# The softmax sums' inverse and division, done at the end of the first slot of a group of four

## The chip, the cores and the metric

The kernel runs on one core of a Trainium2 chip. The metric is the device time of one execution in microseconds (us); lower is better. Below, PE is TensorE, DVE is VectorE, ACT is ScalarE, POOL is GpSimd and SP is SyncE, as the profile names them. L416 is line 416 of the kernel.

## The reference

One block of a conditioned transformer over x of 4 x 1024 x 512, all in fp32: attention with 16 heads of 32, then a gated feed-forward network with 2048 hidden features, and x added once more.

```
def _attention(x, Wq, Wk, Wv, Wo):
    q, k, v = (x @ W.T for each W).reshape(B, L, H, dh)
    attn = jnp.einsum('blhd,bmhd->bhlm', q, k) / scale
    p = jax.nn.softmax(attn, axis=-1)
    o = jnp.einsum('bhlm,bmhd->blhd', p, v).reshape(B, L, D)
    return o @ Wo.T

x = x + _attention(_tc_rmsnorm(x, t, g1w, g1b, b1w, b1b), Wq, Wk, Wv, Wo)
block = x + silu(n @ gate_w.T) * (n @ hid_w.T) @ out_w.T   # n = _tc_rmsnorm(x, t, g2w, ...)
out = x_in + block
```

The change lies in the last step of the softmax: the division of the weighted values by the sum of the exponentials.

## The kernel before, in words

The 4096 tokens are 8 blocks of 512. The attention of a block is 8 groups, each 4 heads by 256 queries over all 1024 keys; a group is 4 slots of 256 keys. So there are 64 groups and 256 slots, and the main loop (L768) runs over a slot number g. I call g % 4 the kind of a slot (0 to 3), the four slots from one of kind 0 a group of slots, and number the 8 groups of slots of a stretch of 32 by position 0 to 7 (position 0 starts at a multiple of 32).

The order of the instructions on PE, DVE, ACT and POOL is written out by hand (`manual_schedule`): it is the order of the calls in this loop. Only SP's DMAs are put in order by a scheduler. Each engine runs its own list in order; where one stands still, all behind it stand.

What one slot does for the attention, with several slots of the pipeline at once:

- `scores(g)` (L310): 16 matmuls of keys and queries into the PSUM tile `sc`; `keep` (L317, ACT) copies it to an SBUF tile `raw`; `running_max` (L322 and L325, DVE) takes the maximum over the keys, in two halves.
- Once a group, in a slot of kind 0, PE transposes the maximum (`mt`, L331), DVE reduces and splits it (L337 to L342); in the next slot, of kind 1, PE transposes that (`pt`, L347), ACT copies it (L349), PE spreads it over the partitions (`sp`, L357), and ACT copies it to the tile `shift` (L358, two halves).
- `shifted(g-5)` (L363, DVE) subtracts it from `raw`: 2048 columns at the beginning of a slot, in kind 1 two halves that wait for `shift`. `exponential(g-5)` (L366, ACT) follows, and in the next slot `weighted` (L376, PE, `av`) multiplies by the values, and `accumulate` (L390) adds up the exponentials with DMAs issued by POOL.
- Three groups of slots after the group's own, in the slot of kind 0, `fold_sum` (L398, DVE) and `sums` (L408, PE) form the sums, and ACT copies them to the tile `total` (L413).
- `inverse` (L416, DVE) is the reciprocal of `total`, and `normalize` (L425, DVE) multiplies the values `avs` by it into `oT`. Both stand at the end of the slot of kind 2, and so on DVE right ahead of `shifted` of the slot of kind 3. For the last group of a block (`j_n % GB == GB - 1`, position 2) they stand at the end of the slot of kind 0, since the output projection needs `oT` then. For group 8 the multiplication comes later (L791).

From slot 60 (`FS`) on, the feed-forward network of the block before is woven in. Each pair of slots forms one of 16 hidden tiles with seven products (a Strassen scheme in two PSUM banks, `pa` and `pb`): `pair_15` and `add_15` (L524, DVE) in the odd slot, then `pair_26` (PE, `pa`), `copy_156` (L539, ACT), `contract` (`pc`, with `take_contract`, L577, DVE), `pair_7`, `sub_5` (L546, DVE) in the even one, then `pair_3`, `gate_tanh` (L556, ACT), `gate` and `hidden` (L561, L564, DVE). All feed-forward matmuls have line 106, that of the helper `mm`. The output projection of a block (`po`) runs at position 2.

Before slot 60 the keys, queries and values of later blocks are projected instead (`pkq`, `pv`), with the norms of their inputs (the reciprocal L632, 128x512, at the end of slots 4, 12, 20, 28, 36 and 44) and sums of weights (L474 to L477). Work listed in `ended` (norms, token sums, weight sums) stands behind the inverse and the division at the end of its slot.

Of the kernel before, what the change touches and what calls it, by code (L numbers as in the profile page):

```python
# [24 lines left out]
def tile_cond_transformer_block(  # L25
# [389 lines left out]
    def inverse(j: int):  # L415
        nc.vector.reciprocal(state["total", j], state["total", j])  # L416

    def normalize(j: int):

        m, qh = divmod(j, NB // HQ)  # L420
        n, hg = divmod(m, C)
        total = state.pop(("total", j))
        if (n, hg) not in oT:
            oT[n, hg] = sb.tile([P, NB], F32, tag=f"oT{hg}", name=f"oT{m}")
        nc.vector.tensor_tensor(oT[n, hg][:, qh * HQ : (qh + 1) * HQ], avs.pop(j), total, ALU.mult)  # L425
# [157 lines left out]
    GB = C * (NB // HQ)  # L583
# [114 lines left out]
    with tc.manual_schedule(  # L698
# [35 lines left out]
        direct = NR // UN - 2  # L734
# [33 lines left out]
        while g < END:  # L768
            kind = g % UN
# [6 lines left out]
            j_n = g // UN - 3  # L776
            n_on = 0 <= j_n < NR // UN
# [84 lines left out]
            else:  # L862
# [34 lines left out]
                    chain(g)()  # L897
                for fn, a in halfway.pop(g, []):
                    fn(*a)
            if kind == 0 and n_on and j_n < direct and j_n % GB == GB - 1:  # L900
                inverse(j_n)
                normalize(j_n)
            if kind == 2 and n_on and j_n < direct and j_n % GB != GB - 1:

                inverse(j_n)
                if j_n != GB:
                    normalize(j_n)
            columns[0] = DH
# [95 lines left out]
```

## Time and profile before

| | us |
|---|---|
| median of 3 runs (lowest, highest) | 2479.35 (2477.35, 2480.38) |
| the profiled execution | 2480.0 |
| its span | 2478.1 |
| PE idle before `av`, for `raw` from ACT | 50.0, in 61 waits |
| PE idle before `pa`, for `pa` from DVE | 8.5, in 43 waits |
| L416 reciprocal, 64 of them | 111.6, 1.744 each |
| L425 multiplication, 64 of them | 27.2, 0.425 each |

A slot is measured on PE, from its first `sc` matmul to that of the next slot. From slot 64 on, each stretch of 32 slots looks like the last; these are slots 128 to 159:

| position | kind 0 | kind 1 | kind 2 | kind 3 |
|---|---|---|---|---|
| 0 | 10.73 | 6.19 | 8.10 | 5.53 |
| 1 | 10.73 | 6.19 | 8.10 | 5.53 |
| 2 | 10.73 | 13.25 | 8.10 | 12.56 |
| 3 | 9.91 | 7.25 | 8.10 | 5.53 |
| 4 | 10.70 | 6.19 | 9.45 | 5.53 |
| 5 | 10.86 | 6.19 | 8.10 | 5.53 |
| 6 | 11.94 | 6.19 | 8.10 | 5.53 |
| 7 | 12.53 | 6.19 | 8.10 | 5.53 |

Position 2 holds the output projection. Before slot 60 the slots of kind 0 from slot 12 on take 12.43, 10.61, 11.22, 11.28, 10.61, 11.28, 11.22, 10.61, 10.60, 12.27, 10.61 and 10.60 us.

How to read it: the profile's timeline has a start and a duration in us for each instruction, and in brackets how long its engine had stood idle before it and who ended that. Starts are counted from the beginning of the span.

### The profile page before, as it was taken

The page shows a single profiled execution, that of the slowest core. Times are in us where ns is not written, and L with a number is a line of the kernel's source. Part 1 is how long each engine was busy: PE and PEld are TensorE (multiplying, and loading weights), DVE is VectorE, ACT ScalarE, POOL GpSimd, SP SyncE. Part 2 cuts the span into 40 slices and gives each one's busy share as a digit, 9 for nine tenths or more (in the row PEclk, how much of TensorE's full clock was granted, in tenths as well). Part 3 has the DMA queues.
Part 4 walks back from the last instruction along what each step waited for, and adds up shares of the span by engine and source line. Part 5 has one row for each costly group of instructions (what it writes and reads, how often), then busy time and mean ns, then how long its engine had stood idle before and what let it go on. Part 6 is the DMA issues. An engine that isn't in the chain of part 4 may idle for free. (4 is left out here: it accounts for less than half of the span.)

```text
span 2478.1 us, 71138 instructions
## 1 busy us (share of the span) xinstructions
PE 2396.0 (97%) x31785; PEld 1121.8 (45%) x31785; DVE 1943.7 (78%) x2180; ACT 1412.4 (57%) x1495; POOL 172.4 (7%) x207
## 2 busy tenths in 40 slices
PE   8999999999999999999999999999999999999999
PEld 3333333344444444444444444444444444444444
DVE  2688888888789988998899978997899889843332
ACT  3677777766566656665666656665666566512111
POOL 0000000000000000000000000000000000000000
PEclk9999999999999999999999999999999999999999
DMA  6599998989878888888888888788788888853432
GB/s 214 178 299 251 265 259 221 238 201 238 197 193 203 203 218 200 200 211 214 207 197 207 226 191 204 199 226 203 196 201 212 210 197 199 201 159 116 138 134 71
DMA packets 185982, 501.69 MB, mean 202 GB/s; under 512 B 21319, under 2 KB 78663, under 8 KB 158286
## 3 DMA queue, kind: packets, MB, share of 16 engines
q0 software_dynamic: 28656, 208.68, 43.6%
q1 hardware_dynamic: 156734, 288.47, 34.2%
q8 instruction: 250, 4.10, 0.6%
q14 instruction: 54, 0.44, 0.1%
q10 hardware_dynamic: 288, 0.01, 0.0%
HBM read 246.44 MB, written 41.97 MB: 116 GB/s over the span
## 5 line engine op out<-in xcount | busy, mean ns | idle before, releaser
L363 DVE TENSOR_TENSOR raw<-raw,shift 128x2048 f32<-128x2048 f32 (+1 forms) x320 | 593.9, 1859 | 65.2 <-ACT shift L358 62.3
L366 ACT ACTIVATE raw<-raw 128x2048 f32<-128x2048 f32 x256 | 490.8, 1917 | 214.3 <-DVE raw L363 213.8
L317 ACT COPY raw<-sc 128x2048 f32<-128x2048 f32 x256 | 479.6, 1873 | 169.9 <-PE sc L310 129.7
L322 DVE TENSOR_TENSOR rmax<-rmax,raw 128x1024 f32<-128x1024 f32 x384 | 469.5, 1223 | 53.9 <-ACT raw L317 48.2
L106 PE MATMUL pc<-h,ow 128*32 128x512 f32 x4096 | 467.7, 593 | 2.1 <-DMA ow<-in_out_w 1.1
L376 PE MATMUL av<-raw,v 128*32 128x256 f32 x4096 | 274.9, 386 | 50.0 <-ACT raw L366 50.0
L390 POOL DMA_DIRECT2D raw<-raw x192 | 165.3, 861 | 1991.5 <-ACT raw L366 939.1
L310 PE MATMUL sc<-q,k 32*128 32x256 f32 x4096 | 293.3, 400 | 0.2 <-ACT raw L317 0.2
L106 PE MATMUL pa<-x,fa 128*32 128x256 f32 x4096 | 270.0, 381 | 8.8 <-DVE pa L524 8.5
L106 PE MATMUL pa<-sums,fw 128*32 128x256 f32 x4096 | 267.9, 379 | 0.0
L106 PEld LDWEIGHTS pc<-h,ow 128*32 128x32 f32 x4096 | 128.2, 110 | 245.5 <-issue 226.7
L310 PEld LDWEIGHTS sc<-q,k 32*128 32x128 f32 x4096 | 184.9, 184 | 116.5 <-issue 81.5
L106 PE MATMUL pkq<-y,wkq 128*32 128x512 f32 (+1 forms) x1664 | 231.3, 594 | 4.2 <-ACT y L196 4.1
L376 PEld LDWEIGHTS av<-raw,v 128*32 128x32 f32 x4096 | 107.2, 109 | 175.8 <-ACT raw L366 88.0
L106 PEld LDWEIGHTS pa<-x,fa 128*32 128x32 f32 x4096 | 127.6, 110 | 124.7 <-DVE pa L524 30.5
L106 PEld LDWEIGHTS pa<-sums,fw 128*32 128x32 f32 x4096 | 133.2, 110 | 88.2 <-issue 0.5
L539 ACT COPY pb<-pa 128x256 f32<-128x256 f32 x128 | 46.2, 361 | 181.4 <-PE pa L106 180.3
L577 DVE SCALAR_TENSOR_TENSOR res<-pc,res 128x512 f32<-128x512 f32 x128 | 88.2, 689 | 67.2 <-PE pc L106 62.9
L556 ACT ACTIVATE t<-pa 128x512 f32<-128x512 f32 x128 | 78.1, 610 | 109.9 <-PE pa L106 109.5
L106 PE MATMUL pa<-x,fw 128*32 128x256 f32 x2048 | 135.2, 381 | 0.0
L106 PE MATMUL pb<-x,fw 128*32 128x256 f32 x2048 | 134.0, 379 | 1.2 <-ACT pb L539 1.2
L106 PE MATMUL pb<-sums,fa 128*32 128x256 f32 x2048 | 133.9, 379 | 0.0
(106 smaller groups left out, 2152.4 us busy)
## 6 DMA issues: line engine op xcount, KB each, us to landing
raw<-raw POOLq DMA_DIRECT2D x192, 1024.0 KB, 9.1
fw<-sw SPq DMA_DIRECT2D x128, 512.0 KB, 7.0
fa<-in_gh_w SPq DMA_DIRECT2D x128, 384.0 KB, 5.9
ow<-in_out_w SPq DMA_DIRECT2D x128, 256.0 KB, 2.9
wkq<-in_kq_w SPq DMA_DIRECT2D x32, 512.0 KB, 5.9
v<-vs SPq DMA_DIRECT2D x128, 128.0 KB, 5.0
k<-kqs SPq DMA_DIRECT2D x124, 128.0 KB, 7.0
kqs<-st SPq DMA_DIRECT2D x61, 256.0 KB, 7.7
```

What stands on the lines that cost most here:

```text
L106: nc.tensor.matmul(dst[k : k + n, :], w[:, k : k + n], moving, start=start, stop=stop, skip_group_check=seeded)
L310: nc.tensor.matmul(sc[:, i, k, :], keys[rows, k * P : (k + 1) * P], queries[rows, :], start=True, stop=True)
L317: nc.scalar.copy(raw[r].rearrange("p k h q -> p h k q"), state.pop(("sc", r)))
L322: nc.vector.tensor_tensor(rmax[j], rmax[j], raw[r][:, k, :, :], ALU.max)
L363: nc.vector.tensor_tensor(t, t, s.unsqueeze(1).to_broadcast(list(t.shape)), ALU.add)
L366: nc.scalar.activation(raw[r], raw[r], AF.Exp)
L376: nc.tensor.matmul(av[j][i * DH : (i + 1) * DH, :], v[m, u][:, k, i * DH : (i + 1) * DH], raw[r][:, k, i, :], start=(kt == 0), stop=(kt == ...
L390: nc.gpsimd.dma_start(out=acc[j].rearrange("p k h q -> p (k h q)"), in_=raw[r].rearrange("p k h q -> p (k h q)"), accum_op=ALU.add,)
L539: nc.scalar.copy(bank_b[p][:, RIGHT], bank_a[p][:, RIGHT])
L556: nc.scalar.activation(state["t", p], bank_a[p], AF.Tanh, scale=0.5)
L577: nc.vector.scalar_tensor_tensor(r, pp, 0.5, r, ALU.mult, ALU.add)
```

## The change

The inverse and the division of every group that is not one of the last two stand at the end of the slot of kind 0, where they stood before only for the last group of each block. The exception of group 8, whose multiplication comes later, stays.

```
-            if kind == 0 and n_on and j_n < direct and j_n % GB == GB - 1:
+            if kind == 0 and n_on and j_n < direct:
                 inverse(j_n)
-                normalize(j_n)
-            if kind == 2 and n_on and j_n < direct and j_n % GB != GB - 1:
-
-                inverse(j_n)
+
                 if j_n != GB:
                     normalize(j_n)
```

In the built programs, the lists of PE, ACT and POOL are in the same order in both kernels. On DVE 55 reciprocals and 54 multiplications move (of group 8 the reciprocal alone). On SP five DMAs change places, all before slot 60: loads of keys and values ahead of stores of weight sums in slots 13 and 37, and one load of keys by one place.

## The prediction

> **What bounds the kernel now.** The page's first part shows PE nearly always busy:
>
> ```profile
> PE 2396.0 (97%) x31785; PEld 1121.8 (45%) x31785; DVE 1943.7 (78%) x2180; ACT 1412.4 (57%) x1495; POOL 172.4 (7%) x207
> ```
>
> What a change on DVE can win is PE's idle time. I therefore read the waits next, PE's first:
>
> ```profile
> PE av L376 <- ACT raw L366: 50.0, 61, 2.6
> PE pa L106 <- DVE pa L524: 8.5, 43, 0.2
> ```
>
> 58.5 us of PE's 82 idle us (2478.1 - 2396.0) end with an exponential, or with the sum that stands behind the maximum on DVE. Splitting these waits by slot gives 28.0 and 8.3 us to the slots of kind 0 from slot 60 on, 5.4 to those of kind 0 before slot 60, 12.5 to those of kind 2, 4.2 to the slots after the last scores. The timeline shows what a kind-0 wait comes from; slot 103 is of kind 3, position 1. DVE, then ACT, then PE:
>
> ```profile
> 878.33 1.74 DVE L416 RECIPROCAL total<-total 128x256 f32<-128x256 f32 x1
> 880.10 0.42 DVE L425 TENSOR_TENSOR oT<-avs,total 128x256 f32<-128x256 f32 x1
> 880.45 2.29 DVE L363 TENSOR_TENSOR raw<-raw,shift 128x2048 f32<-128x2048 f32 x1
> ```
>
> ```profile
> 882.77 1.91 ACT L366 ACTIVATE raw<-raw 128x2048 f32<-128x2048 f32 x1 [1.34 <-DVE raw L363]
> ```
>
> ```profile
> 883.28 1.15 PE L310 MATMUL sc<-q,k 32*128 32x256 f32 x16
> 884.73 1.07 PE L376 MATMUL av<-raw,v 128*32 128x256 f32 x16 [0.30 <-ACT raw L366]
> ```
>
> The pair stands straight ahead of the subtraction; ACT has idled 1.34 us for it; PE waits for ACT. No instruction between is free to overtake. So the bound is PE, plus once per group the chain DVE, ACT, PE of kind 3.
>
> **What leaves kind 3.** The pair occupies DVE from 878.33 to where the next instruction starts, 880.45: 2.12 us. Without it the subtraction ends at 880.62 instead of 882.74. ACT then waits only for its tanh (880.83 + 0.60), so the exponential starts at 881.43 and ends at 883.34, and PE comes to `av` at 884.36 by itself: 1.0 us to spare. The sum L524 (885.52 to 885.94) moves by 2.12 to 883.82, when PE wants it at 885.24: to spare too.
>
> How much does the slot shrink? The trace has the slot without the pair ahead of it: position 3, since position 2 has its pair in kind 0. The windows view of a kind-0 slot at position 2 (pair in the kind 3 before) and at position 3 (not):
>
> ```profile
> 883.28:894.01 10.73, 10.23 (x134) 4.69 (x130) 10.26 (x15) 6.07 (x6) 0.86 (x1) 1.00 0.97 250
> 927.92:937.83 9.91, 9.91 (x134) 4.87 (x131) 8.38 (x12) 5.55 (x6) 1.72 (x2) 1.00 1.03 231
> ```
>
> Columns: length, then busy PE, PEld, DVE and so on. 134 matmuls in both, DVE 96% busy against 85%. The slot is 0.82 us shorter, of which only 0.50 is recorded idle; PE also looks 0.32 us busier after a wait. I take lengths, not gaps.
>
> [...]
>
> With 9.91 as the free length, the gains of kind 0 by position in the table above are 0.82, 0.82, 0.82, 0, 0.79, 0.95, 2.03. Position 6 (11.94) has two `norm_scale` (1.28 together) behind the pair in kind 2; without the pair its exponential ends at 0.47 into the slot, before PE's 1.08. Position 7 (12.53) has token sums in the chain; there `fold_sum` would end about 4.24 us into the slot, where PE wants it at 3.69, so I take 9.91 + 0.65 = 10.56 and a gain of 1.97. Sum per 32 slots: 8.20.
>
> **What arrives in kind 1.** The end of a kind-0 slot on DVE is followed by the subtraction of kind 1, in two halves. DVE, slot 101 (no pair) and slot 105 (position 2, pair already there):
>
> ```profile
> 865.52 2.50 DVE L363 TENSOR_TENSOR raw<-raw,shift 128x1024 f32<-128x1024 f32 x2 [1.64 <-ACT shift L358]
> ...
> 894.34 1.74 DVE L416 RECIPROCAL total<-total 128x256 f32<-128x256 f32 x1
> 896.12 0.42 DVE L425 TENSOR_TENSOR oT<-avs,total 128x256 f32<-128x256 f32 x1
> 896.46 1.22 DVE L363 TENSOR_TENSOR raw<-raw,shift 128x1024 f32<-128x1024 f32 x1
> ```
>
> Slot 101 starts at 863.46, slot 105 at 894.01: the subtraction starts 2.06 and 2.45 us in. The idle 1.64 us take most of the pair's 2.12; the two halves end at 4.55 and 4.80. The exponential starts at 5.21 in both (868.67 and 899.22), because ACT copies `sc` and `avs` first. So in a plain group the pair costs nothing, with 0.4 us to spare. This is a measured twin, seven times in the trace.
>
> Not so where other work already fills that idle time, as the pair goes ahead of it. Only what is left of the idle time and the spare before ACT is cover then. PE reaches `av` 1.08 us into kind 2, and the exponential, starting at 5.21, ends 0.96 in: only 0.1 to spare there.
>
> - Position 6: two `norm_scale` (329 to 1611 ns into slot 121). They end at 3.73, the halves at 6.01, the exponential at 7.99, that is 1.80 into kind 2; `av` 0.78 late.
> - Position 7: a token sum (0.68); exponential ends 1.20 in; 0.18 late.
> - Position 3: norm sums, but that slot is 7.25 long; ends 0.94 in; nothing.
> - Position 4's wait of 1.28 in kind 2 is ACT's table load; it stays.
>
> So 0.96 per 32 slots, net 8.20 - 0.96 = 7.24; six stretches (slots 64 to 255): **-43.4**.
>
> **Before slot 60.** Here the end of kind 0 holds the long reciprocal of the norm:
>
> ```profile
> 214.00 3.35 DVE L632 RECIPROCAL tota<-tota 128x512 f32<-128x512 f32 x1
> 217.26 1.16 DVE L363 TENSOR_TENSOR raw<-raw,shift 128x1024 f32<-128x1024 f32 x1
> ```
>
> DVE has no gap left (slot 21 starts at 214.37); the halves end at 5.19, the exponential starts at 5.22. Pushed by 2.12 it ends 3.09 into slot 22, `av` 2.07 late. Slots 12, 20, 28, 36 do this: 2.12 + 2.07 + 2.07 + 2.12. Slot 44 moves the reciprocal alone: 1.6. Slot 48 (weight and norm sums) 1.2, slot 24 (weight sums) 0.36, slots 56 and 60 0.18 and 0.16. Loss 11.9. Gains are the kind-0 slots over the free 10.61: slots 20, 24, 32, 36 by 0.61, 0.67, 0.67, 0.61, slot 48 by 1.66; slot 12's wait has no pair ahead. Gain 4.2. Net **+7.7**.
>
> **After the last scores.** Slot 256 loses its wait of 1.38 and what hangs on it (-1.5); slot 257 has no copies on ACT to hide the pair (+1.15); slot 259 loses 2.1 of its 2.56. Net **-2.4**.
>
> The moved pair issues no DMA. Of the five moved on SP, loads go ahead of stores that would now wait longer; I count nothing, with 2 us either way. On DVE the reciprocal waits for L413, which ends 0.8 us before at the least (slot 48): nothing. `oT` is needed five slots later or more. Sum: -43.4 + 7.7 - 2.4 = -38.1; from the profiled 2480.0, 2441.9, and the median of the runs lies 0.65 below that execution, within its spread. I say **2442**.
>
> [...]
>
> **Rivals.**
>
> [...]
> 2. The slot shrinks only by the recorded gap (0.5, not 0.82): 6 positions by 0.32, six times, 11.5 less: 2454. For it: position 3 follows the long slots of the projection, so DVE starts it with less behind. Against: the same 134 matmuls.
> 3. The early waits are absorbed, since DVE and PE are late by the same amount and kind 2 loses its pair: half of the 11.9 goes, 2436. Against: in these slots PE waits at once.
> 4. Transfers bound instead. DMA share is 0.97 to 1.03 in the rows above, and at position 2 the last accumulation lands 4.1 us before its fold, which the change takes 1.3 earlier. It would need groups to keep their 30.5 us: no change, 2480. Against: PE waits 1.1 us for a DMA in the whole trace.
>
> That nothing moves is excluded by the order of the built programs.
>
> **Numbers.** Forecast 0.65, rival 1 0.06, rival 2 0.16, rival 3 0.09, rival 4 0.04. Range 2432 to 2458: from rival 3 to rival 2, with the 2 us of SP and the 1.5 us by which the runs spread added at both ends. 0.2% (5 us) is what a measurement can tell from no change. Faster 0.90, same 0.04, slower 0.06.
>
> **What would show it.** Right: kind-0 slots of 9.9 us at positions 0 to 6, no `av` wait in them, kind 1 still 6.19; in kind 2 new waits of 0.8 at position 6, and of 2 in slots 14, 22, 30, 38. Wrong: `av` waits in kind 2 of plain positions, reciprocals over 1.75, or `fold_sum` waiting for a DMA.

## The result, and the profile after

| | before | after |
|---|---|---|
| median of the runs, us | 2479.34 | 2451.15 |
| lowest, highest | 2477.35, 2480.38 | 2447.08, 2453.34 |
| the profiled execution | 2480.0 | 2447.08 |
| its span | 2478.1 | 2445.3 |

The ratio of the times is 0.9887, with an interval of 0.9875 to 0.9899. The change wins 28 us where 37 were forecast. The four runs after the change lie 6.3 us apart, at 2447.1, 2449.2, 2453.1 and 2453.3, and the profiled one is the lowest: its trace holds less than the median has to tell.

The page's first part and then the view of waits, PE's rows, of the kernel after (line, what it waited for, us in total, times, longest):

```profile
PE 2386.7 (98%) x31785; PEld 1128.7 (46%) x31785; DVE 1938.9 (79%) x2180; ACT 1416.2 (58%) x1495; POOL 172.8 (7%) x207
```

```profile
PE av L376 <- ACT raw L366: 30.6, 24, 3.5
...
PE av L376 <- ACT totf L151: 3.3, 6, 0.6
```

The waits of `av` for the exponential fell from 50.0 us in 61 times to 30.6 in 24, and PE's wait for `pa` on DVE, 8.5 us before, is down to 0.2. But the longest wait of the first row is now 3.5 us, and a row is new: `av` waits six times 0.55 us for a copy of a norm (L151). The prediction has neither.

The windows view, at slots 104 and 108 (kind 0 of positions 2 and 3, the two slots that the prediction set side by side) and slot 110 (kind 2 of position 3). Columns: length, then busy PE, PEld, DVE, ACT, POOL with instructions, granted PE clock (share of full speed), DMA share, GB/s:

```profile
888.47:898.38 9.91, 9.91 (x134) 4.87 (x130) 8.57 (x13) 4.73 (x5) 0.86 (x1) 1.00 0.92 248
932.29:942.20 9.91, 9.91 (x134) 4.87 (x130) 8.38 (x12) 5.56 (x6) 1.72 (x2) 1.00 1.03 229
949.45:958.17 8.72, 8.17 (x116) 3.74 (x112) 8.06 (x9) 6.18 (x7) 0.62 (x1) 1.00 0.38 134
```

Slot 104 took 10.73 before; now it is the twin of slot 108. Slot 110 took 8.10 and is now 8.72 long, with PE busy for 8.17.

The difference of the two profiled executions by stretch of slots, against the prediction's terms (us):

| stretch | predicted | measured |
|---|---|---|
| start to slot 0 | 0 | +0.35 |
| slots 0 to 63 | +7.7 | +12.06 |
| slots 64 to 254 | -43.4 | -40.04 |
| slot 255 to the end | -2.4 | -5.20 |
| sum | -38.1 | -32.83 |
| median of the runs, from that execution | -0.65 (of before) | +4.07 (of after) |

So there are three errors to explain: 4.4 us early, 3.4 us in the long part, and some 5 us by which the runs differ, against 2.8 us won unforeseen at the end.

### The profile page after: what moved, and what is told of

The parts are those of the page before. It is cut to its first block, busy times and chain, and to the rows that moved or that the text cites. A ratio compares the mean times of both kernels' runs of the same rounds, so it can differ in the third digit from the quotient of the medians.

```text
span 2445.3 us, 71149 instructions
## 1 busy us (share of the span) xinstructions
PE 2386.7 (98%) x31785; PEld 1128.7 (46%) x31785; DVE 1938.9 (79%) x2180; ACT 1416.2 (58%) x1495; POOL 172.8 (7%) x207
## 5 line engine op out<-in xcount | busy, mean ns | idle before, releaser
L363 DVE TENSOR_TENSOR raw<-raw,shift 128x2048 f32<-128x2048 f32 (+1 forms) x320 | 589.0, 1856 | 3.3 <-ACT shift L358 2.8
L376 PE MATMUL av<-raw,v 128*32 128x256 f32 x4096 | 275.8, 387 | 34.5 <-ACT raw L366 30.6
L106 PEld LDWEIGHTS pkq<-y,wkq 128*32 128x32 f32 (+1 forms) x1664 | 73.2, 118 | 131.5 <-issue 118.3
```

What stands on the lines that cost most here:

```text
L106: nc.tensor.matmul(dst[k : k + n, :], w[:, k : k + n], moving, start=start, stop=stop, skip_group_check=seeded)
L363: nc.vector.tensor_tensor(t, t, s.unsqueeze(1).to_broadcast(list(t.shape)), ALU.add)
L376: nc.tensor.matmul(av[j][i * DH : (i + 1) * DH, :], v[m, u][:, k, i * DH : (i + 1) * DH], raw[r][:, k, i, :], start=(kt == 0), stop=(kt == ...
```

## Experiments

"The pair" is, as in the prediction, the reciprocal and the multiplication. In each expectation "Theory A" is the account held to be right at that point, and the rivals stand beside it.

### e1 and e2: one half of the change each

e1 moves the pair from slot 60 on alone (`FS` is 60), e2 is its mirror (`g < FS` and `g >= FS` exchanged) and moves it before slot 60 alone:

```
-            if kind == 0 and n_on and j_n < direct:
+            if kind == 0 and n_on and j_n < direct and (j_n % GB == GB - 1 or g >= FS):
                 inverse(j_n)
                 if j_n != GB:
                     normalize(j_n)
+            if kind == 2 and n_on and j_n < direct and (j_n % GB != GB - 1 and g < FS):
+                inverse(j_n)
+                if j_n != GB:
+                    normalize(j_n)
```

> The pair stands in kind 0 only from slot 60 on; before slot 60 it stays in kind 2, as in the kernel before. Theory A: slots 12 to 63 cost the change 12.1 us in its profiled run, 7.2 by waits and 4.9 by three stretches of 3.4 us at half TensorE clock that waits of 2 us and more set off. Then slots 0 to 63 take what they took before, the profiled execution is near 2447.1 - 12.1 = 2435, the clock returns to 0.998 and the runs lie within 3 us of each other. Theory B: the lower clock and the spread of 6 us come from the denser feed-forward part. Then 2439 to 2441, clock 0.995 to 0.997, spread still 6 us.

> The mirror: the pair stands in kind 0 only before slot 60, later it stays in kind 2. Theory A: slower by 10 to 17 us (2489 to 2496 against 2479), with clocks of 0.995 to 0.997 and a spread of some 6 us. Theory B: slower by 7 to 8 us, clock 0.998, spread 3 us as before. If the early part were harmless: 2479.

Measured: e1 2439.21 us (2435.64 to 2446.61; ratio 0.9846, 0.9831 to 0.9861), e2 2489.29 (2488.50 to 2491.67; ratio 1.0045, 1.0033 to 1.0058). Slots 0 to 63 cost +0.14 us in e1 and +11.94 in e2, slots 64 to 254 -39.70 and +0.12: the two halves add up to the change, and the early half is a loss by itself. The loss is larger than the 7.7 of the prediction. Slots 14, 22 and 38 grew by 3.42, 3.76 and 3.66 us in the kernel after, where 2.1 us each were forecast; slot 30, with a wait as long as slot 22's, grew by 2.07 as forecast.

The windows view of the kernel after shows what differs. Each pair of rows is a wait's stretch of 3.41 us and the next one, for slots 14, 22 and 30:

```profile
156.01:159.42 3.41, 0.66 (x15) 0.25 (x8) 3.38 (x4) 1.25 (x1) 0.10 (x1) 1.00 1.12 312
159.42:162.83 3.41, 2.70 (x24) 1.12 (x28) 3.41 (x3) 2.97 (x4) 0.00 (x0) 0.50 1.00 219
224.27:227.69 3.42, 1.43 (x28) 0.70 (x24) 3.35 (x5) 2.83 (x3) 0.00 (x0) 1.00 1.03 231
227.69:231.10 3.41, 3.41 (x20) 0.87 (x16) 3.38 (x5) 1.39 (x2) 0.00 (x0) 0.50 0.97 303
...
292.54:295.95 3.41, 1.73 (x24) 0.81 (x28) 3.38 (x3) 3.41 (x3) 0.00 (x0) 1.00 1.03 221
295.95:299.37 3.42, 3.42 (x36) 1.04 (x32) 3.39 (x4) 2.96 (x3) 0.30 (x1) 1.00 0.69 247
```

Behind the waits of slots 14 and 22 the granted clock is 0.50 for 3.41 us (and behind slot 38's at 360.8 us); behind slot 30's it is 1.00. In e2 the same three slots drop, at the same times within 0.1 us. At half clock half the work is done: in the two stretches with PE busy throughout, 16 `pkq` matmuls start in that from 227.69 and 32 in that from 295.95. So up to 1.7 us, half of 3.41, are lost each time; the three slots lost 1.30, 1.69 and 1.54 over the forecast, 4.5 us in all, and 7.7 + 4.5 is 12.2. Which wait is followed by half clock is not fixed by the order of the early slots: e5 and e10 below have the same early order and the same waits, and there slot 14's wait is followed by two stretches at half clock (from 158.31 in e5), slot 22's by none and slot 38's by one; slots 0 to 63 cost 11.85 and 11.95 us.

That leaves e1's spread: its profiled run is the lowest (2435.64), and one run took 11 us more. It has no early waits, so the early clock can't be the cause.

### e3: the copy that holds the bank

Why does slot 110 wait? The timeline of the kernel after, ACT and PE at the start of that slot (in brackets the idle time before an instruction and who ended it):

```profile
948.44 1.91 ACT L366 ACTIVATE raw<-raw 128x2048 f32<-128x2048 f32 x1 [0.90 <-DVE raw L363]
...
950.25 0.35 ACT L520 COPY p<-pa 128x256 f32<-128x256 f32 x1
950.51 0.59 ACT L151 COPY totf<-pmf 128x512 f32<-128x512 f32 x1
...
951.15 1.07 PE L376 MATMUL av<-raw,v 128*32 128x256 f32 x16 [0.55 <-ACT totf L151]
```

The exponential ended at 950.35, in time for PE at 950.60. But at this position `norm_mean` has put its sums `pm` into the one PSUM bank that `av` uses, and the copy L151 that frees it stands on ACT behind the exponential, which ends 0.90 us into the slot; before, it ended 0.10 us ahead of the slot, and L151 ended 0.64 us in, before PE came to `av` at 1.08. ACT in the kernel before (slot 110 starts at 945.07):

```profile
943.03 1.94 ACT L366 ACTIVATE raw<-raw 128x2048 f32<-128x2048 f32 x1
944.85 0.38 ACT L520 COPY p<-pa 128x256 f32<-128x256 f32 x1
945.10 0.62 ACT L151 COPY totf<-pmf 128x512 f32<-128x512 f32 x1
```

The expectation below tests that by putting the copy, which comes from the `amid` list, ahead of that of take_5 (L520):

```
                 pair_15(p + 1)
-                take_5(p + 1)
                 for fn, a in amid.pop(g, []):
                     fn(*a)
+                take_5(p + 1)
```

> The changed kernel, with the copy of the mean (L151, which frees the PSUM bank that av needs) ahead of the copy take_5 (L520) on ACT in slots of kind 1 at position 3. Theory A: the 0.55 us wait of av in kind 2 at position 3 ends with that copy, so it falls to about 0.2 and the slot from 8.72 to about 8.4; six times, 2 us in all. Theory B: av waits there for the exponential, which stays where it is: 8.72 unchanged.

The same place in e3:

```profile
950.41 0.57 ACT L151 COPY totf<-pmf 128x512 f32<-128x512 f32 x1
...
951.03 1.07 PE L376 MATMUL av<-raw,v 128*32 128x256 f32 x16 [0.28 <-ACT totf L151]
```

The wait is halved and the slot is 8.45 long, in all six slots of this kind: `av` starts when this copy has ended, so the bank is the cause. The time did not follow: 2453.95 us (2450.91 to 2454.91; ratio 0.9897, 0.9882 to 0.9912). Slots 64 to 254 are 0.87 us better than after the change (six times 0.27 is 1.6, and slot 208 is 0.69 longer), but from slot 255 on e3's profiled run is 8.3 us worse. Something there outweighs what is measured.

### e4: the multiplication behind the subtraction

From slot 60 on the reciprocal stays at the end of kind 0, and the multiplication (0.425 us) goes behind both halves of the subtraction in kind 1; before slot 60 as in e1. Position 2 keeps both in kind 0.

```
+            if kind == 1 and ("split", j_n) in state:
+                state.pop(("split", j_n))
+                normalize(j_n)
...
                 inverse(j_n)
-                if j_n != GB:
-                    normalize(j_n)
+                if j_n % GB == GB - 1:
+                    normalize(j_n)
+                else:
+                    state["split", j_n] = True
```

> As the first kernel here (kind 2 before slot 60), and from slot 60 on only the reciprocal stands at the end of kind 0; the multiplication follows the two halves of the subtraction in kind 1, where DVE waits 0.3 to 0.5 us for the copy of the scores anyway. Theory A: the halves come 0.34 us earlier than with the pair, so kind 2 falls at position 6 from 8.84 to about 8.5, at position 3 from 8.72 to about 8.4, at position 7 to 8.10; five us less than the first kernel, near 2430. Theory B: the multiplication delays the maximum and what follows it, and nothing is won: 2435 or more.

Measured: 2436.51 us (2432.18 to 2438.67; ratio 0.9829, 0.9815 to 0.9842). In kind 2, position 3 is 8.20 long (8.72 after), position 7 8.10 (8.23), position 6 about 8.6 (8.84): with 0.42 us less on the path, each wait shrinks by 0.1 to 0.5. Slots 64 to 254 win 45.95 us over before. Yet the median lies only 2.7 us below e1's. The profiled run shows where that went. DVE and PE after the last scores, from the timeline of e4:

```profile
2151.69 1.23 DVE L398 TENSOR_TENSOR raw<-raw 128x1024 f32<-128x1024 f32 x1 [7.92 <-DMA raw<-raw]
```

```profile
2153.02 1.08 PE L408 MATMUL sum<-raw,ones_sum 128*32 128x256 f32 x8 [7.92 <-DVE raw L398]
```

The last group's `fold_sum` waits 7.92 us for a DMA, and PE's sum behind it as long. The clock in the 6.8 us from 2150.0 on, by the windows view of e4:

```profile
2150.00:2156.80 6.80, 3.30 (x20) 0.82 (x24) 3.40 (x3) 0.37 (x1) 0.00 (x0) 0.50 0.03 10
```

The DMA is the last of the three `accumulate` DMAs of that group, which add into one tile and run one after the other (in the rows below, POOL idles 13.22 us for the second before it issues the third). e3 has the same wait (7.62 us, then 6.8 us of half clock). Where do the times of these DMAs come from? First SP's, then POOL's instructions in e4:

```profile
2115.80 1.02 SPq L579 DMA_DIRECT2D out<-res  x1
...
2125.91 0.33 SPq L429 DMA_DIRECT2D res<-in_x  x1
```

```profile
2126.21 0.86 POOL L390 DMA_DIRECT2D raw<-raw  x1 [9.90 <-DMA raw<-raw]
2140.29 0.86 POOL L390 DMA_DIRECT2D raw<-raw  x1 [13.22 <-DMA raw<-raw]
```

And the same in the kernel after:

```profile
2133.79 0.34 SPq L579 DMA_DIRECT2D out<-res  x1
...
2136.65 0.62 SPq L429 DMA_DIRECT2D res<-in_x  x1
```

```profile
2143.63 0.86 POOL L390 DMA_DIRECT2D raw<-raw  x1 [9.34 <-DMA raw<-raw]
2153.81 0.86 POOL L390 DMA_DIRECT2D raw<-raw  x1 [9.32 <-ACT pb L539]
```

(The third DMA starts when the second has landed, at 2153.3; the releaser that the row names is not the last.) In e4 the load of `res` (1 MB) starts 0.3 us before the second accumulation, which then takes 13.6 us; in the kernel after it has started 7 us before, and the accumulation takes 9.7. In all seven traces of kernels with these DMAs (before, after, e1 to e4, e8), the second accumulation took 13.6 or 13.7 us in the three whose load began 37.9 to 38.4 us after slot 255's start, and 9.6 to 11.0 in the four whose load began at 31.1 to 32.4. In the three the load began 0.3 to 0.7 us before that accumulation, in the four 6.5 to 7.3 us before it. That is a correlation; what starts the load early or late was not isolated. The times go with it: of the four runs each, the profiled one is the highest in e3 and e4, which have the long wait, and the lowest in the kernel after and in e1, which do not.

### e5, e6, e7: the last group without these DMAs

If that chain makes the runs differ, they must agree without it. The last group's exponentials are added up by DVE, where `running_max` no longer runs:

```
         if u == 0:
             acc[j] = raw[r]
+        elif j == NR // UN - 1:
+            state["add"] = r
         else:
...
+    def add_last():
+        if "add" in state:
+            r = state.pop("add")
+            t = acc[r // UN]
+            nc.vector.tensor_tensor(t, t, raw[r], ALU.add)
...
                 if g < NR:
                     running_max(g, 0)
                     running_max(g, 1)
+                add_last()
...
```

(The last `...` stands for the same call for the odd slots.) e5 is the kernel after with this, e6 the kernel before, e7 that of e4.

> The kernel after the change, but the exponentials of the last group (slots 253 to 255) are added up by three DVE additions of 128x2048 in slots 259 to 261, where running_max no longer runs, in place of the three POOL DMAs. Theory A: the change has brought the last group's slots so far forward that its chain of three serial accumulation DMAs (8 to 13 us each) ends last in some executions, and costs a wait of up to 7 us before the last sum and some 3 us of half clock behind it; that is what most runs of the changed kernel have over its profiled one. Then no wait stands before the last sum, the last folding starts some 15 us earlier, and the runs lie at 2444 to 2449 us, median near 2446. Rival B: the runs differ through the half-clock stretches of the early slots alone; then the median stays at 2450 to 2452, with runs to 2453. Rival C: the three additions (6.8 us of DVE) make PE wait in slots 259 to 261 and cost 2 to 6 us: 2449 to 2457, with new waits there.

> The same three DVE additions in the kernel before the change. Theory A: there the last fold came only 1 us late, since the last group's slots were slower, so little is to be won: 2475 to 2478 us, 1 to 3 under the kernel before. Rival: the kernel before loses as much to these DMAs as the one after; then 2470 to 2473. If the additions themselves cost time, 2480 to 2484.

> The three DVE additions in the kernel of e4_mult_later, whose profiled execution (2438.7 at most, 2432.2 at least over its runs) waited 7.9 us before the last sum and then ran 6.8 us at half clock. Theory A: without that wait 2426 to 2430 us, with runs within 3 us. Rival B (the runs differ through something else): 2434 to 2437.

| | median (lowest to highest), us | ratio to before |
|---|---|---|
| e5 | 2446.10 (2445.61 to 2446.99) | 0.9871 (0.9856 to 0.9886) |
| e6 | 2478.22 (2476.78 to 2479.19) | 1.0000 (0.9991 to 1.0009) |
| e7 | 2427.72 (2427.51 to 2428.56) | 0.9797 (0.9783 to 0.9810) |

The three additions, in e7's timeline, DVE (L402 is the new line, L363 the subtraction):

```profile
2117.29 2.28 DVE L402 TENSOR_TENSOR raw<-raw,raw 128x2048 f32<-128x2048 f32 x1
...
2126.47 2.29 DVE L402 TENSOR_TENSOR raw<-raw,raw 128x2048 f32<-128x2048 f32 x1
...
2129.61 2.28 DVE L402 TENSOR_TENSOR raw<-raw,raw 128x2048 f32<-128x2048 f32 x1
```

The last ends at 2131.9, against 2151.7 in e4 where the DMA let the fold start. The runs of e5 lie 1.4 us apart instead of 6.3, those of e7 1.1 instead of 6.5, and e7's median falls by 8.8 us. Rivals B and C fall; in e5's profile the additions lengthen one slot, 260, by 0.37 us. In the kernel before nothing is won, where 1 to 3 us were expected: its slots after the last scores are slower, and the same DMA of 13.7 us costs it a wait of 1.03 us. So the change turned a chain that was nearly hidden into one that ends last in some executions, at a cost of 4 to 5 us in the median (2451.15 to 2446.10). Medians of different groups of runs can be compared to about 1 us only: the kernel before had 2479.34 beside the kernel after, 2478.46 beside e1 to e4, 2478.67 beside e5 to e8 and 2477.67 beside e9 and e10. e7 is the fastest kernel of the study.

### e8: a shorter early wait

Before slot 60 the reciprocal alone moves; elsewhere the kernel is that of before.

```
+            if kind == 0 and n_on and j_n < direct and j_n % GB != GB - 1 and g < FS:
+                inverse(j_n)
             if kind == 2 and n_on and j_n < direct and j_n % GB != GB - 1:
-                inverse(j_n)
+                if g >= FS:
+                    inverse(j_n)
```

> The kernel before the change, but in slots before 60 the reciprocal alone stands at the end of kind 0; the multiplication stays in kind 2. Theory A: PE then waits about 1.6 us in slots 14, 22, 30 and 38 in place of 2.0 to 2.1. The step itself costs 5 to 7 us less 3 to 4 won in kind 0; if a half-clock stretch needs a wait of about 2 us, none follows slots 14, 22 and 38: 2481 to 2484 us. If a wait of 1.6 us sets off the stretches as well, 4 to 5 us more: 2485 to 2489. Rival: the reciprocal overlaps the long one of the norm without a new wait; then 2475 to 2478.

Measured: 2485.69 us (2482.86 to 2486.81; ratio 1.0026, 1.0015 to 1.0037), in two bunches, 2483 and 2486. In the profiled run slots 22 and 30 grow by 1.55 us each, without half clock; slots 14 and 38, with 1.34 us of waiting there before, wait 2.95 us, drop to half clock (0.50) and grow by 3.16 and 3.30. So neither branch of the expectation holds for all slots: the length of the added wait alone does not tell where half clock follows. In the traces it goes with how long PE was busy in the whole stretch of 3.41 us: 1.43 us or less (last section).

### e9 and e10: e1 and e3 again, without the DMA wait

> The kernel of e1_late_only (the pair in kind 0 only from slot 60 on) with the three DVE additions in place of the last group's POOL DMAs. Theory A: without the DMA wait the runs lie within 3 us; against e5_tail_after (2446.1) the loss of the slots before 60 (12.1 us in the profiled run) is gone: 2433 to 2435 us. Against e7_tail_split (2427.7) it lacks only the later multiplication, which by the slots of kind 2 is worth about 6 x 0.9 us. Rival: the spread of e1_late_only (2435.6 to 2446.6) had another cause and stays; then the median is 2437 to 2440 with runs over 2442.

> The kernel of e3_copy_first with the three DVE additions. Theory A: the copy that frees the bank ahead of take_5's copies wins 0.28 us in kind 2 of position 3, six times, against e5_tail_after (2446.1): 2443 to 2446 us. If the copies of take_5 that now come later make PE wait elsewhere, or if the bank was not the cause, 2446 to 2450.

Measured: e9 2434.16 us (2433.72 to 2434.79; ratio 0.9821, 0.9806 to 0.9835), e10 2444.75 (2442.91 to 2445.09; ratio 0.9861, 0.9845 to 0.9878). The spread of e1 is gone. Now two parts can be read from medians, to about 1 us: the early slots cost 2446.10 - 2434.16 = 11.9 us, and the multiplication on the path of kind 1 costs 2434.16 - 2427.72 = 6.4, where the slots gave 6.2 in the profiles. The order of the copy gives 1.35, less than these medians can tell apart with certainty; what it is worth is read from the slots (slots 64 to 254 are 1.27 us shorter in e10's profile than in e5's).

## Why the prediction was right, and where it failed

- **What leaves kind 3** was right. Kind 0 is 9.91 us at positions 0 to 6 wherever no other work comes in, and 10.48 at position 7 (10.56 forecast). PE's busy share of 97% was no obstacle: 0.82 us a group came, as the slot's length said. Rival 2 (0.50 a group) is excluded.
- **What arrives in kind 1** was right: 6.19 us as before, so kind 1 did not turn into the bound (rival 1, given 0.06): 15 of the 64 reciprocals overlap a DMA issue of POOL in the trace after, and all last 1.741 to 1.754. e1's gain of 39.7 us shows it over all the slots. In kind 2, position 6 waits 0.74 more (0.78 forecast), position 7 0.14 (0.18).
- **The pair's 2.12 us on DVE** were right: behind slot 104 in the trace after, the reciprocal starts at 898.71 and the subtraction behind the pair at 900.83. The means are those of before, 1.744 and 0.425 us.
- **"Position 3: ends 0.94 in; nothing"** failed. The step looked at the exponential alone. `av` needs its data and its PSUM bank, and the bank was freed by L151 behind it on ACT. The term of 0 is +0.62, six times: 3.7 of the 3.4 us missed in the long part, the rest of the sum being 0.3 better. e3 and e10 show the cause.
- **"Before slot 60 ... Loss 11.9"** failed in its size. The added waits came where and as long as forecast, the gains too (0.62 to 0.68 in slots 20, 24, 32 and 36; 1.54 in 48). But a wait was priced at its length, and in slots 14, 22 and 38 it also took the granted clock to half for 3.41 us. The term of +7.7 measured +12.1, and e2 shows it alone. Rival 3, that these waits are absorbed, is excluded.
- **After the last scores** the profiled gain was 5.2, not 2.4. Counted from the first `av` matmul of a slot to that of the next, slot 255 won 1.45 (the wait of 1.38 that the prediction gives to slot 256), slot 256 0.32 and slot 259 2.12; slot 257 lost 0.71 where 1.15 was forecast; and slot 260, which was not in the sum, won 1.66. That last gain is the clock again, and partly luck: in the profiled run before, the wait of 2.56 us just ahead of slot 260's `av` was followed by a stretch at half clock. The windows view of the kernel before:

```profile
2166.01:2169.42 3.41, 0.86 (x17) 0.26 (x8) 2.03 (x2) 1.95 (x2) 0.00 (x0) 1.00 1.14 206
2169.42:2172.84 3.42, 3.40 (x32) 1.55 (x36) 3.16 (x4) 0.22 (x1) 0.86 (x1) 0.50 0.60 186
```

The same happened in e6, but not in e2 and e8, which have the same wait. After the change 0.44 us of the wait are left, and no half clock follows. Not foreseen was that the last group's accumulations keep their pace while the slots shrink (the second took 13.7 us before, 13.6 or 13.7 in e3 and e4, and 9.7 in the profiled run after). That is the mechanism of **rival 4**, set aside because "PE waits 1.1 us for a DMA in the whole trace", but in one place instead of in every group. The waits view of the kernel before had rows that would have led there, PE's and DVE's:

```profile
PE sum L408 <- DVE raw L398: 1.0, 1, 1.0
```

```profile
DVE raw L398 <- DMA raw<-raw: 1.0, 1, 1.0
```

The last `sum` waits 1.03 us for the last fold, with a DMA behind it: a chain without slack, in a stretch about to be shortened. It makes the median of the runs 4 to 5 us worse (e5). At position 2, where the prediction looked for rival 4, the last accumulation still lands 0.86 us before its fold at the least, 4.10 before the change; the slack shrank by more than the 1.3 us forecast, but held.

From 2441.9 these terms lead to the median: + 4.4 early, + 3.4 in the long part, - 2.8 at the end, + 0.35 at the start, + 4.07 from the profiled run to the median, together 2451.3. The first and last of these are shown by e2 with e9 and by e5; how the DMAs ended in the unprofiled runs is inferred from e5's agreement. That 2451 lies within the range is no merit of the range: it was drawn from rival 3 to rival 2, and neither occurred.

## What to carry over

A move is priced at the place where it lands, and everything that place waits for counts: the data, the bank that has to come free, the transfer that was hidden. When a stretch gets shorter, look for the chain in it that keeps its own pace, here three DMAs in series, and look beside the profiled run at the spread of the others. Where one region of a kernel gains and another loses from the same edit, make the edit in the first alone: e9 wins about 12 us over e5 with one condition.

## What the runs showed of the hardware

- In the traces the granted clock was 1.00 or 0.50 and changed in steps of 3.413 us: in the kernel after, the drops at 159.42, 227.69 and 360.81 us lie 20 and 39 steps apart. In the twelve traces, from full clock from 35 us on and until 20 us before the end, each stretch in which PE was busy for 1.43 us or less was followed by one at half clock, and none with 1.48 us or more was (in the kernel after, 0.66, 1.43 and 0.20 us ahead of the three drops, and 1.73 us or more elsewhere). (Before 35 us it was otherwise: in the kernel after, PE was busy for 2.77 us of the stretch from 33.12, and half clock followed.) A gap of 1.99 us was followed by half clock when it lay within one stretch (224.82 to 226.82 in slot 22 of the kernel after, PE busy for 1.43 us of it) and was not when a boundary fell into it (292.23 to 294.22, slot 30, PE busy for 3.10 and 1.73 us of the two stretches). The boundaries have no fixed place in the kernel: the same wait of slot 14 is followed by half clock from 159.42 us in the kernel after and from 158.31 in e5. The stretches are counted from each trace's own drops.
- In the traces half clock lasted one stretch or two. Two, 6.8 us, followed waits of 7.6 and 7.9 us (e3, e4), but also slot 14's wait of 3.46 us in e5 and e10; in the kernel after that wait was followed by one. After 35 us a half-clock stretch with PE busy for 2.48 us or less was followed by another, and none with 2.70 us or more was.
- In the last group, the second `accumulate` DMA of 1 MB took 13.6 to 13.7 us in the three traces where another load of 1 MB began 0.3 to 0.7 us before it, and 9.6 to 11.0 in the four where that load began 6.5 to 7.3 us before it. That the load is the cause was not tested. All 192 of them in the kernel after took 7.0 to 13.9 us.
